# Encoder attention of a four-layer graph network: one-bank sum tiles, four row-term buffers, five blocks masked a part earlier, and a bfloat16 mask

## The chip, the cores and the metric

The kernel runs on one core of a Trainium2 chip, in one launch. The metric is the device time of a run in microseconds (us); less is better. The trace gives the time on a clock that starts with the span of one profiled execution. The engines are named as in the profile: PE (TensorE's matrix multiplications; PEld loads its weights), DVE (VectorE), ACT (ScalarE), POOL (GpSimd) and SP (SyncE, which here only issues DMAs). L469 is line 469 of the kernel before.

## The reference

Four residual layers on N = 2708 nodes with 512 features, over one dense 0/1 adjacency `adj` of 2708 x 2708; each is followed by a layer norm. Only the first one's attention matters here. It has four heads of 128 features, and the call passes `adj` for both patterns, so the two masked softmaxes are equal:

```python
Xw = jnp.einsum('hnd,hde->hne', Xh, W)
f1 = jnp.einsum('hnd,hd->hn', Xw, V[:, 0, :, 0])
f2 = jnp.einsum('hnd,hd->hn', Xw, V[:, 1, :, 0])
sig = jax.nn.sigmoid(f1[:, :, None] + f2[:, None, :])
...
local_att = _masked_softmax(local_pattern[None] * sig, lmask)
...
Xa = jnp.einsum('hij,hjd->hid', att, Xw)
```

After it come a batch norm, a block with a matrix multiplication, a decoder that uses the same `att`, and the layers 1 to 3, which the change leaves alone.

## The kernel before

**Tiling.** Everything is float32. The attention is computed transposed: the neighbours j lie on the 128 partitions, the nodes i along the free dimension. The nodes are cut into two halves of 1354 (`HSPAN`), the heads into two pairs, which makes four *parts* in the order `PARTS` = (half 0, pair 0), (0, 1), (1, 0), (1, 1). In every part a loop goes over 22 blocks of 128 neighbours (`ORDER`; one block has only 20 rows and stands in the middle). So there are 88 steps (`STEPS`), k = 0 to 87, and parts begin at 0, 22, 44 and 66.

**One step** has these pieces:

- A DMA on SP loads the block of `adj`, transposed (`adjT`), into a tile `a` of 128 x 1354 (four buffers). For pair 0 this is the raw 0/1 block, and it is masked (*prepared*): L423 writes z = (a == 0) into one tile `z`, L424 adds z times -1e30 to `a`, both on DVE, and a DMA on POOL's queue stores the result in `adj_d` in DRAM. For pair 1 the masked block is loaded back from `adj_d`.
- `tanhs` (L369): two ACT operations, tanh((f1 + f2) / 2), one for each head. f2 is the bias of each partition. f1, the *row term*, is read from a tile `f1b` of 128 x 1354, in which one row is spread to all partitions.
- `arguments` (L364): one DVE operation over both heads, (t + 1) times `a`.
- `exponentials` (L440): one ACT operation over both heads. For some blocks the result is stored for the decoder (`kept`, 1.35 MB, POOL's queue).
- `node_sums` (L469): for each head 11 matrix multiplications, one for each 128 nodes, with the exponentials as weights and 129 columns of values (the last is 1 and gives the softmax's sum). A float32 multiplication leaves two records, so a step has 44. They run two steps behind (`FRONT`).

**Sums.** The 11 results of a head need four PSUM banks (three to a bank), so two heads fill all eight. They are kept in three tiles `po0`, `po1`, `po2` of two banks each, which hold bank 0, 1 and 2 of both heads, and two tiles `psm0`, `psm1` of one bank for the last two results of each head. All of PSUM belongs to one pool, `ps_a`; the opening work uses the same tiles.

**Change of parts.** After the last sums of a part, `keep` evicts the eight banks on DVE (L684 takes a maximum, L685 a reciprocal, L686 writes the scaled `rows`), which only then leaves PSUM to the next part. Its function `turn` then transposes the rows on PE (L705, L713), again through the four banks `po[1]` of head 1, and copies them into `ft` on DVE or ACT (L726); `sm` goes to `rs_d` for the decoder. Until the transposes of both heads are done (`turns`), the new part's sums stand back (`waiting`). Statistics of `ft` (L728) are computed later, one in a step, in parts with pair 1 (`later`). After part 4 the evicted rows are transposed in the closing work, beside a few products of the weights of layer 3.

**Row terms.** Three buffers of tag `f1b` are turned over. Each part takes two; the buffer that a part's second tile takes was used until the last `tanhs` of the part before:

```python
                    with behind(loads[-9]):
                        nc.sync.dma_start(state["f1b"][0][:, :w], f1[:, 0, :])
                    nc.scalar.dma_start(state["f1b"][1][:, :w], f1[:, 1, :])
```

The first is loaded on SP's queue, the second on ACT's own. The row terms themselves are made at the start: `f1_rows` copies (L273) a chunk of 452 or 450 nodes out of PSUM. The three chunks of the first half are needed at once. The three of the second half come in `rest`, after the arguments of step 0: each is copied into a tile `f1c` (tag `rs`, two buffers) and stored to `f1_d` by a DMA on POOL's queue.

**Order.** Tile pools hand out buffers and insert the waits; a scheduler orders instructions on each engine by priority, and `behind(x)` or `tc.issue_after(x)` holds a group back behind a given instruction. The mask of step k stands behind the arguments of step k - 2 (`args[-2:-1]`), the arguments behind the previous ones, the `tanhs` behind the exponential of step k - 2.

## Time and profile before

| | us |
|---|---|
| median of 3 runs (3160.28 to 3168.04) | 3165.48 |
| the profiled execution | 3166.74 |
| its span in the trace | 3164.9 |
| up to the first steps (0 to 38.4 of the trace) | 38.4 |
| the 88 steps, until the last sum (38.4 to 528.4) | 490.0 |
| everything after it (closing work, decoder, layers 1 to 3) | 2636.5 |

Over the whole span PE is busy 3091.0 us (98%), DVE 2042.2 (65%), ACT 1368.7 (43%) and POOL 161.5 (5%). That average mixes stages: within the 88 steps PE is busy 453.0 of 490.0 us, DVE 392.4 and ACT 440.9, afterwards PE 2607.2 of 2636.5. An answer such as `L273 ... [6.25 <-DMA f_d<-f1c]` reads: line, engine, operation, output <- input with shapes, and in brackets how long the engine had been idle just before and what ended this (here a DMA that reads `f1c` and writes `f_d`, which is the trace's name for `f1_d`). In the timeline the line begins with start and duration in us.

### The profile page before, as it was taken

What the parts mean: (1) busy time and instruction counts of PE and PEld (TensorE: products, weight loads), DVE (VectorE), ACT (ScalarE), POOL (GpSimd) and SP (SyncE); (2) the same over time, 40 slices, a digit from 0 to 9 for tenths busy, and PEclk for the clock granted to TensorE, in tenths of its full rate; (3) what the DMA queues carried; (4) which work ended last, traced back from release to release, by engine and by line L of the source; (5) the groups of instructions that cost most, each with busy time, mean ns of one, the idle gap of its engine ahead of it and who ended that gap; (6) DMA issues with size and microseconds to landing.
All of it is one profiled execution on the core that took longest, in us unless ns stands there. A gap on an engine that the chain in (4) does not pass through costs nothing.

```text
span 3164.9 us, 39531 instructions
## 1 busy us (share of the span) xinstructions
PE 3091.0 (98%) x15144; PEld 2352.3 (74%) x15144; DVE 2042.2 (65%) x3807; ACT 1368.7 (43%) x1652; POOL 161.5 (5%) x282
## 2 busy tenths in 40 slices
PE   8999999999999999999999999999999999999999
PEld 7889988444444446885578888777768888888886
DVE  6968966876786685444266667777545555555565
ACT  6989988677867451001133333434301111111111
POOL 1100100000000000000011110000110000000000
PEclk9999999999999999999999999999999999999999
DMA  8866865156545413541154445556431111111110
GB/s 259 304 225 246 286 241 183 70 190 211 178 174 195 164 60 105 145 125 38 45 150 141 139 147 146 163 176 177 131 98 40 50 53 50 50 50 50 50 48 32
DMA packets 204307, 426.07 MB, mean 135 GB/s; under 512 B 21342, under 2 KB 135106, under 8 KB 198294
## 3 DMA queue, kind: packets, MB, share of 16 engines
q1 hardware_dynamic: 180126, 320.19, 33.1%
q0 software_dynamic: 23552, 101.26, 8.9%
q8 instruction: 119, 1.95, 0.3%
q10 hardware_dynamic: 440, 2.10, 0.2%
q14 instruction: 70, 0.57, 0.1%
HBM read 326.14 MB, written 95.87 MB: 133 GB/s over the span
## 4 chain that ended last, share of the span: by engine, by line
PE 72%; DVE 9%; ACT 9%; issue 7%; DMA 3%; POOL 0%; SPq 0%; DVEq 0%; POOLq 0%; ACTq 0%
PE po L1629 19%; PE ps_s L1424 18%; PE po L567 9%; PE ps_nb L1227 7%; PE ps_wide L1277 4%; ACT t L440 4%; DVE t L364 4%; ACT t L369 3%; PE po L469 3%; PE ps_hid L131 2%; PE ps_sup L1835 2%; PE ps_v L131 2%; PE ps_dec L994 2%; DMA f1b<-f_d 1%; PE ps_mlp L865 1%
## 5 line engine op out<-in xcount | busy, mean ns | idle before, releaser
L364 DVE SCALAR_TENSOR_TENSOR t<-t,a 128x2708 f32<-128x2708 f32 (+1 forms) x152 | 452.3, 2978 | 183.0 <-ACT t L369 178.4
L469 PE MATMUL po<-xw,t 128*128 128x129 f32 (+2 forms) x3872 | 448.5, 283 | 37.0 <-ACT t L440 21.8
L469 PEld LDWEIGHTS po<-xw,t 128*128 128x128 f32 (+2 forms) x3872 | 439.7, 193 | 45.4 <-ACT t L440 27.5
L369 ACT ACTIVATE t<-f1b,f2h 128x1354 f32<-128x1354 f32 (+1 forms) x304 | 415.8, 1413 | 43.5 <-PE po L567 32.8
L1424 PE MATMUL ps_s<-q,hT 128*128 128x256 f32 (+1 forms) x1848 | 405.5, 372 | 0.0
L1629 PE MATMUL po<-sup,e 128*128 128x256 f32 (+1 forms) x1512 | 398.3, 384 | 5.5 <-DVE c L1710 2.8
L567 PE MATMUL po<-t,emb 128*128 128x452 f32 (+3 forms) x1056 | 397.7, 545 | 4.4 <-ACT t L552 4.2
L1424 PEld LDWEIGHTS ps_s<-q,hT 128*128 128x128 f32 x1848 | 339.2, 190 | 49.8 <-issue 5.1
L567 PEld LDWEIGHTS po<-t,emb 128*128 128x128 f32 (+1 forms) x1056 | 193.4, 190 | 201.7 <-issue 188.4
L1629 PEld LDWEIGHTS po<-sup,e 128*128 128x128 f32 (+1 forms) x1512 | 264.4, 185 | 59.9 <-issue 19.4
L1629 PE MATMUL po<-held,T 128*128 128x256 f32 x1200 | 293.7, 380 | 0.0
L1629 PEld LDWEIGHTS po<-held,T 128*128 128x128 f32 x1200 | 226.8, 190 | 31.4 <-issue 0.9
L2030 DVE SCALAR_TENSOR_TENSOR e<-a_cols,ps_s 128x512 f32<-128x512 f32 (+1 forms) x121 | 79.9, 660 | 233.2 <-PE ps_s L1424 229.4
L440 ACT ACTIVATE t<-t 128x2708 f32<-128x2708 f32 x88 | 216.0, 2455 | 20.7 <-DVE t L364 20.0
L1424 PE MATMUL ps_s<-hT 128*128 128x256 f32 (+2 forms) x968 | 213.8, 372 | 0.7 <-ACT sup L1842 0.7
L1424 PEld LDWEIGHTS ps_s<-hT 128*128 128x128 f32 x968 | 175.0, 190 | 29.2 <-issue 4.3
L1227 PE MATMUL ps_nb<-hid_hi,at 128*128 128x512 f32 x484 | 185.5, 390 | 0.4 <-DVE at L1219 0.4
L552 ACT ACTIVATE t<-t 128x2708 f32<-128x2708 f32 x64 | 157.4, 2459 | 60.4 <-DVE t L364 60.2
L1227 PE MATMUL ps_nb<-hid_lo,at 128*128 128x512 f32 x462 | 179.9, 389 | 0.0
L1932 ACT ACTIVATE a_score<-a_score,neg_big 128x512 f32<-128x512 f32 (+3 forms) x131 | 88.6, 684 | 190.5 <-DMA a_score<-in_adjT_dram 95.7
L2022 ACT ACTIVATE q<-ps_wide,uq 128x256 f32<-128x256 f32 (+1 forms) x44 | 20.5, 466 | 335.7 <-PE ps_wide L1277 335.7
L1534 ACT ACTIVATE e<-e 128x512 f32<-128x512 f32 (+1 forms) x187 | 114.1, 617 | 118.1 <-DVE e L1533 117.8
(269 smaller groups left out, 3989.0 us busy)
## 6 DMA issues: line engine op xcount, KB each, us to landing
a<-adj_d SPq DMA_DIRECT2D x108, 677.0 KB
a_cols<-in_adjT_dram SPq DMA_DIRECT2D x200, 256.0 KB
a<-in_adjT_dram SPq DMA_DIRECT2D x42, 677.0 KB
adj_d<-a POOLq DMA_DIRECT2D x42, 677.0 KB, 5.5
kept<-t POOLq DMA_DIRECT2D x20, 1354.0 KB, 7.2
t<-kept SPq DMA_DIRECT2D x20, 1354.0 KB
raw<-in_adjT_dram SPq DMA_DIRECT2D x105, 256.0 KB
a_score<-in_adjT_dram SPq DMA_DIRECT2D x55, 256.0 KB
```

Source lines behind the costliest of these rows:

```text
L131: nc.tensor.matmul(ps[:n], xt[:, c, :n], w[:, c, :], start=(c == 0), stop=(c == C - 1))
L364: return nc.vector.scalar_tensor_tensor(t, t, GUARD, ab, ALU.add, ALU.mult)
L369: done = nc.scalar.activation(t[:, k, :], f1b[k][:n, :w], AF.Tanh, bias=f2h[:n, jt, h : h + 1], scale=0.5,)
L440: nc.scalar.activation(t[:rows, :, :w], t[:rows, :, :w], AF.Exp, scale=0.5)
L469: nc.tensor.matmul(po[k][b][:m, s * DR : (s + 1) * DR], t[own : own + n, k, i0 : i0 + m], values[own : own + n, jt, HP * p + k, :], start= ...
L552: nc.scalar.activation(t, t, AF.Exp, scale=0.5)
L567: nc.tensor.matmul(po[HB * k + q][:, :qw], values[r : r + n, jt, h * P : (h + 1) * P], t[r : r + n, k, q0 : q0 + qw], start=(place == 0), ...
L1227: nc.tensor.matmul(pos[it][:n], at, half[:, jt, :], start=(jt == 0 and k == 0), stop=(jt == NT - 1),)
L1277: nc.tensor.matmul(ps[:, :width], w(c, o), xt(c), start=(c == 0), stop=(c == C - 1),)
L1424: nc.tensor.matmul(ps[:, jb, i:w], keys[:, c, j : j + P], st["q"][:, c, i:], start=(c == 0), stop=(c == C - 1),)
L1534: return nc.scalar.activation(e, e, AF.Exp)
L1629: nc.tensor.matmul(po[bank][rows, half, :], lhsT, rhs, start=(k == 0 and half == 0) if first is None else first, stop=last, skip_group_che ...
```

## The change

It has five parts.

1. *Sums in eight one-bank tiles.* The opening work's PSUM pool is now `ps_p`. `banks()`, called after step 0's arguments, closes it and makes a pool `ps_a` with one tile for each bank of each head.
2. *Four row-term buffers.* `f1_tile` has two tags, `f1b0` and `f1b1`, of two buffers each; parts alternate between them. Both loads of a part are on SP's queue, behind the load of `a` three before.
3. *Row terms of the second half at the start.* The three chunks are copied into one tile `later_rows`, which is a spare `f1b1` buffer, and leave with one store instead of three.
4. *Mask.* `z` is bfloat16. The mask of step k stands behind the arguments of step k - 1 instead of k - 2.
5. *Five blocks of the second half masked during part 2.* At places 1, 4, 7, 10, 13 of part 2 `fetch_early` loads the raw block that is needed at place 2, 6, 10, 14, 18 of part 3 into a buffer of tag `f1b0`, whose tiles are idle in part 2. Three places later it is masked, behind the latest arguments, and stored to `adj_d`. In part 3 these five are loaded from `adj_d`, masked already.

The closing work's loads of `bq` and of one weight block move to tag `f1b0`. The diff, cut to its core:

```diff
...
     KEPT = [(8, 11, 14, 18), (1, 4, 7, 9, 11, 14, 17, 20)]
     KEPT = [[ORDER[k] for k in places] for places in KEPT]
+    EARLY = [1, 4, 7, 10, 13]
+    PREPARED = [ORDER[k] for k in (2, 6, 10, 14, 18)]
+    assert all(BLOCKS[jt][1] == P for jt in PREPARED)
     zeros = const.tile([P, NT, NHALF], F32, name="zeros")
     nc.vector.memset(zeros, 0.0)
     dram = ctx.enter_context(tc.tile_pool(name="dram", bufs=1, space=bass.MemoryType.DRAM))
...
         nc.vector.memset(xw[:, :, :, P:], 1.0)
         xT_sb = feat_tile("xT_sb")
 
+        def f1_tile(att, odd, name="f1b"):
+            return att.tile([P, HW], F32, tag=f"f1b{odd}", name=name, bufs=HP)
+
         def load_mlp(w, name):
             t = pf.tile([P, C, F], F32, tag="mlp_w", name=name)
             nc.sync.dma_start(t, w.rearrange("(c p) o -> p c o", p=P))
...
             nc.vector.tensor_copy(wv1, w0x[:, :, P : P + 1].to_broadcast([P, H, 32]))
 
-            stage, *f1b = [
-                att.tile([P, HW], F32, tag="f1b", name=name, bufs=HP + 1)
-                for name in ["f1_rows"] + ["f1b"] * HP
-            ]
+            stage, later_rows = [f1_tile(att, 1, name) for name in ("f1_rows", "f1_later")]
+            f1b = [f1_tile(att, 0) for _ in range(HP)]
             def f1_rows(ci, dst):
                 c0, w = CHUNKS[ci]
...
                 with tc.issue_after(step.ins):
                     for jt in range(AT_ONCE, NT):
                         values_of(jt)
-                    for ci in range(HB, NCH):
-                        c0, w = CHUNKS[ci]
-                        f1c = att.tile([P, BW], F32, tag="rs", name="f1c")
-                        f1_rows(ci, f1c)
-                        nc.gpsimd.dma_start(f1_d[:, c0 : c0 + w], f1c[0 : 32 * H : 32, :w])
+                    h0, w = HSPAN[1]
+                    for q, (q0, _) in enumerate(HCH[1]):
+                        f1_rows(HB + q, later_rows[:, q0:])
+                    nc.gpsimd.dma_start(f1_d[:, h0 : h0 + w], later_rows[0 : 32 * H : 32, :w])
                     copies(xw[:, NT - 1].rearrange("p h e -> p (h e)"))
                     copies(f2h[:, NT - 1, :])
                     nc.vector.tensor_scalar(bm1, prm_sb[:, MB_DEC, :], 1.0, None, ALU.subtract)
...
         PARTS = [(hf, p) for hf in range(NHALF) for p in range(H // HP)]
         STEPS = [(part, place) for part in PARTS for place in range(NT)]
 
-        def encoder_pass(values, att, psum, finish, f1b, blocks, spread, rest):
+        def encoder_pass(values, att, banks, finish, f1b, blocks, spread, rest):
             FRONT = 2
-            tanh, args, exps, tiles, loads = [], [], [], [], []
+            tanh, args, exps, tiles, loads, fetched = [], [], [], [], [], []
             state = {"f1b": f1b}
             def rows_of(k):
...
                 n = BLOCKS[jt][1]
                 return hf, p, jt, n if n == P else HR
 
+            def mask_block(a, hf, jt, rows, *after):
+
+                h0, w = HSPAN[hf]
+                j0, n = BLOCKS[jt]
+                z = att.tile([P, HW], BF16, tag="z", name="z", bufs=1)
+                with behind(*after):
+                    nc.vector.tensor_scalar(z[:rows, :w], a[:rows, :w], 0.0, None, ALU.is_equal)
+                done = nc.vector.scalar_tensor_tensor(
+                    a[:rows, :w], z[:rows, :w], -BIG, a[:rows, :w], ALU.mult, ALU.add
+                )
+                nc.gpsimd.dma_start(adj_d[j0 : j0 + n, h0 : h0 + w], a[:n, :w])
+                return done
+
+            def fetch_early(jt):
+
+                j0, n = BLOCKS[jt]
+                h0, w = HSPAN[1]
+                a = f1_tile(att, 0, "a_early")
+                with behind(loads[-1]):
+                    nc.sync.dma_start(a[:n, :w], adjT[j0 : j0 + n, h0 : h0 + w])
+                fetched.append((a, jt))
+
             def open_step(k):
                 hf, p, jt, rows = rows_of(k)
                 h0, w = HSPAN[hf]
                 j0, n = BLOCKS[jt]
-                prepare = p == 0
+                done_early = hf > 0 and jt in PREPARED
+                prepare = p == 0 and not done_early
                 if STEPS[k][1] == 0 and k > 0:
                     f1 = f1_d[HP * p : HP * (p + 1), h0 : h0 + w].partition_broadcast(P)
-                    state["f1b"] = [
-                        att.tile([P, HW], F32, tag="f1b", name="f1b", bufs=HP + 1)
-                        for _ in range(HP)
-                    ]
-                    with behind(loads[-9]):
-                        nc.sync.dma_start(state["f1b"][0][:, :w], f1[:, 0, :])
-                    nc.scalar.dma_start(state["f1b"][1][:, :w], f1[:, 1, :])
+                    state["f1b"] = [f1_tile(att, k // NT % 2) for _ in range(HP)]
+                    with behind(loads[-3]):
+                        for i in range(HP):
+                            nc.sync.dma_start(state["f1b"][i][:, :w], f1[:, i, :])
                 t = wide_tile(att, "t")[:, : HP * HW].rearrange("p (k w) -> p k w", k=HP)
                 src = adjT if prepare else adj_d
                 if k < len(blocks):
...
                 if n < P:
                     load_few(a, src, h0, w)
                 if prepare:
-                    z = att.tile([P, HW], F32, tag="z", name="z", bufs=1)
-                    with behind(*args[-2:-1]):
-                        nc.vector.tensor_scalar(z[:rows, :w], a[:rows, :w], 0.0, None, ALU.is_equal)
-                    nc.vector.scalar_tensor_tensor(
-                        a[:rows, :w], z[:rows, :w], -BIG, a[:rows, :w], ALU.mult, ALU.add
-                    )
-                    nc.gpsimd.dma_start(adj_d[j0 : j0 + n, h0 : h0 + w], a[:n, :w])
+                    mask_block(a, hf, jt, rows, *args[-1:])
                 tiles.append((t, a))
                 with behind(*exps[k - 2 : k - 1] if k > 1 else tanh[-1:]):
                     tanh.append(tanhs(t[:rows, :, :w], state["f1b"], hf, p, jt, rows, w))
...
                         skip_group_check=True,
                     )
 
-            both = [
-                psum.tile([P, HP, BANK], F32, tag=f"po{q}", name="po", bufs=1) for q in range(HB)
-            ]
-            more = [
-                psum.tile([P, BANK], F32, tag=f"psm{k}", name="po", bufs=1) for k in range(HP)
-            ]
-            po = [[both[q][:, k, :] for q in range(HB)] + [more[k]] for k in range(HP)]
-
             later, turns, waiting = [], [], []
             for k in range(len(STEPS) + FRONT):
                 inside, pending = k < len(STEPS), len(turns)
...
                     form(k)
                     if k == 0:
                         rest(args[0])
+                        po = banks()
                 if k >= FRONT:
                     part, place = STEPS[k - FRONT]
                     t, _ = tiles[k - FRONT]
...
                     exponentials(k - 1, *copies_done)
                 if inside and pending:
                     form(k, *copies_done if not scalar else [])
+                place = k - NT
+                if place - 3 in EARLY:
+                    a, jt = fetched.pop(0)
+                    args.append(mask_block(a, 1, jt, P, args[-1]))
+                if place in EARLY:
+                    fetch_early(PREPARED[EARLY.index(place)])
         def decoder_pass(values, att, psum, finish):
 
...
         less = p0.tile([P, C], F32, name="enc_less")
         with (
             tc.tile_pool(name="att_a", bufs=2) as att,
-            tc.tile_pool(name="ps_a", bufs=1, space=PSUM) as psum,
+            ExitStack() as sums,
         ):
+            first = ExitStack()
+            psum = first.enter_context(tc.tile_pool(name="ps_p", bufs=1, space=PSUM))
             f1b, blocks, spread, rest = project(att, psum)
+
+            def banks():
+
+                first.close()
+                pool = sums.enter_context(tc.tile_pool(name="ps_a", bufs=1, space=PSUM))
+                own = [
+                    [pool.tile([P, BANK], F32, name=f"po{k}{b}") for b in [HB, *range(HB)]]
+                    for k in range(HP)
+                ]
+                return [tiles[1:] + tiles[:1] for tiles in own]
+
             mlp_w, last_po, last_later, last_turn = [], [], [], []
             ft = feat_tile("ft")
 
...
                     return []
                 return [lambda *a, k=k: whole(k, *a) for k in range(HP)]
 
-            encoder_pass(xw, att, psum, keep, f1b, blocks, spread, rest)
+            encoder_pass(xw, att, banks, keep, f1b, blocks, spread, rest)
             emb = rows_tile("emb")
             room = emb[:, NT - 2 * C :, :]
             wqT, wkT = room[:, :C, :], room[:, C:, :]
...
             raws = []
             for name, w in (("wq", wq), ("wk", wk)):
                 for part in range(2):
-                    tag = "z" if len(raws) == 3 else "a"
-                    t = att.tile([P, HW], F32, tag=tag, name=name, bufs=1 if tag == "z" else 4)
+                    if len(raws) == 3:
+                        t = f1_tile(att, 0, name)
+                    else:
+                        t = att.tile([P, HW], F32, tag="a", name=name, bufs=4)
                     t = t[:, : half * F].rearrange("p (c o) -> p c o", c=half)
                     nc.sync.dma_start(
                         t,
...
                         ),
                     )
                     raws.append(t)
-            bq = att.tile([P, HW], F32, tag="f1b", name="bq", bufs=HP + 1)
+            bq = f1_tile(att, 0, "bq")
             nc.sync.dma_start(
                 bq[:, :F], bq_d.rearrange("c p -> (c p)").partition_broadcast(P)
             )
```

## Prediction

> **What bounds the kernel now.** The change touches only the encoder attention, so after the page I asked for busy time by stage: part 1 with its start, part 2, part 3, part 4, each cut where TensorE's sums run on without a gap after the change of parts.
>
> ```profile
> span 3164.9 us, 39531 instructions
> 38.40:184.20 145.80, 126.05 (x1038) 121.46 (x1038) 127.22 (x106) 119.13 (x73) 17.93 (x33) 0.93 0.78 261
> 184.20:301.30 117.10, 111.70 (x994) 110.99 (x993) 85.29 (x72) 112.85 (x73) 7.90 (x15) 0.97 0.68 241
> 301.30:426.90 125.60, 115.13 (x995) 113.11 (x993) 113.03 (x95) 112.01 (x70) 14.86 (x27) 0.96 0.77 276
> 426.90:528.40 101.50, 100.11 (x907) 99.68 (x906) 66.82 (x46) 96.88 (x60) 4.75 (x9) 0.98 0.60 208
> ```
>
> The columns are length, then PE, PEld, DVE, ACT and POOL busy, PE's clock, DMA share, GB/s. No engine has much room: the stage cannot gain more than some 10%, and DVE has slack only in parts 2 and 4. Next, who waits for whom in 38 to 530 us:
>
> ```profile
> ACT ft L726 <- PE po L705: 12.8, 4, 5.9
> PE po L469 <- DVE rows L686: 9.3, 3, 4.0
> ACT t L369 <- DMA f1b<-f_d: 8.9, 3, 4.2
> DVE f1c L273 <- DMA f_d<-f1c: 6.2, 1, 6.2
> ```
>
> All four sit at the start or where parts change. The timeline shows the pace between: first part 1, then part 2.
>
> ```profile
> 131.48 0.86 DVE L423 TENSOR_SCALAR z<-a 128x1354 f32<-128x1354 f32 x1
> 131.60 2.46 ACT L440 ACTIVATE t<-t 128x2708 f32<-128x2708 f32 x1 [0.47 <-DVE t L364]
> 132.38 1.57 DVE L424 SCALAR_TENSOR_TENSOR a<-z,a 128x1354 f32<-128x1354 f32 x1
> 134.08 2.98 DVE L364 SCALAR_TENSOR_TENSOR t<-t,a 128x2708 f32<-128x2708 f32 x1
> ...
> 195.01 2.45 ACT L440 ACTIVATE t<-t 128x2708 f32<-128x2708 f32 x1
> 195.14 2.98 DVE L364 SCALAR_TENSOR_TENSOR t<-t,a 128x2708 f32<-128x2708 f32 x1 [2.00 <-ACT t L369]
> ```
>
> In part 1 DVE is the bound: 0.86 + 1.57 + 2.98 and gaps make 5.49 us a step (128.59 to 134.08). In part 2, unmasked, ACT is: one exponential and two tanh, 4.98 us a step (190.03 to 195.01), and DVE idles 2.00 us in each. PE needs 44 records, under 4.94 us. Part 3 starts at ACT's pace, because the preceding slack let DVE mask ahead, and falls to DVE's later: exponentials at 342.85 and 347.83, but at 385.09 and 390.65. In all parts the last exponential is 8.4 us ahead of the last sum (519.9 against 528.35); I take that as kept, so what ACT gains, the end gains.
>
> **The change part by part.** I number the 88 steps 0 to 87, so that parts begin at 0, 22, 44, 66.
>
> Start. The third copy of the later rows waits for a buffer:
>
> ```profile
> 48.49 0.63 DVE L273 COPY f1c<-pf 128x450 f32<-128x450 f32 x1 [6.25 <-DMA f_d<-f1c]
> ```
>
> It now writes into a tile of its own, and that wait is gone. Not all is won: in the new order on DVE the mask of step 1 comes only after the arguments of step 0, where it had been free at 25.62. From 38.55 on: mask, the last copies, mask end at 42.45; arguments of step 1 to 45.5, mask of step 2, arguments of step 2 at 47.95 instead of 51.60: **3.6 gained**. Bounds: 6.2 if the mask hides again, 1 if step 1's store, now behind the row stores on POOL's queue, holds up a load (that load would land near 55, its mask is due near 62).
>
> Part 1's pace stays; the mask now writes bfloat16. The nearest rows are
>
> ```profile
> L942 DVE TENSOR_SCALAR linked<-rb 128x1354 bf16<-128x1354 f32 x2 | 1.9, 928 | 10.2 <-DMA rb<-rs_d 10.2
> L532 DVE TENSOR_SCALAR_CACHE_REDUCE z<-a 128x1354 uint8<-128x1354 f32 x42 | 65.6, 1562 | 3.5 <-DMA a<-adj_d 3.5
> ```
>
> The first is the same kind of compare from float32 to bfloat16, 0.88 and 0.98 us against 0.86; the second also sums, which explains its time. I take +0.04 for 21 masks: **-0.8**. Bounds per mask: 0 and +0.70. The second operation reads bfloat16 and float32, and I leave its 1.57.
>
> First change of parts (step 22). Now:
>
> ```profile
> 161.33 1.42 ACT L369 ACTIVATE t<-f1b,f2h 128x1354 f32<-128x1354 f32 x1 [3.91 <-DMA f1b<-f_d]
> ...
> 170.67 0.16 DVE L684 TENSOR_SCALAR rc<-po 128x3 f32<-128x3 f32 x1
> ...
> 174.61 4.26 PE L469 MATMUL po<-xw,t 128*128 128x129 f32 x22 [2.64 <-DVE rows L686]
> ...
> 185.03 2.47 ACT L440 ACTIVATE t<-t 128x2708 f32<-128x2708 f32 x1
> ```
>
> With four row buffers both loads are issued on SP some six steps ahead (0.7 MB each, 9.4 us at worst, two loads of `a` behind them, each with about 13 us to spare). The exponential of step 21 then starts at 159.15 instead of 162.66, and the arguments of step 23 end at 167.3 instead of 170.7, where the evictions start. They took 6.3 us; PE resumed 3.9 us after their start, when bank 0 of both heads was free. With one tile a bank it resumes after the first bank, 1.15 us in. The new order then interleaves transposes and copies: following it bank by bank with the evictions' spacing, the arguments of step 24 start 7.95 us after the evictions (10.7 before), PE runs on from 10.0 (13.5 before), and the exponential of step 24 starts at 11.75, that is at 179.05 instead of 185.03. **6.0**, of which I keep 5.5, because PE's clock fell after the gap shown above (windows of 2 us, clock third from the right):
>
> ```profile
> 172.00:174.00 2.00, 0.00 (x0) 0.00 (x0) 2.00 (x15) 2.00 (x2) 0.00 (x0) 1.00 0.79 303
> 176.00:178.00 2.00, 2.00 (x11) 2.00 (x10) 0.87 (x6) 1.70 (x2) 0.00 (x0) 0.50 0.83 347
> ```
>
> The clock halved after 2.64 us of idling, and 22 records took 4.26 us against 2.69 warm; the remaining gap is 1.9 us, for which no row decides, so the bounds are 0 and -1.6 at each change. [...]
>
> Part 2 takes on five masks of part 3. Each is 2.45 us on DVE where 2.00 is idle, so the next arguments start 0.45 late, 1.2 where a 0.69 us statistic lies in the same step. The exponential has 2.0 us of slack after its arguments (4.98 - 2.98), so I cost them at **0**; without that cover five times 1.2. Their DMAs: ten of 0.68 MB in 110 us, on a share of 0.68 where part 1 runs at 0.78. A fetch from the third on waits on SP for the store of the mask two before it, with later loads of `a` queued behind: issue is held by up to 5 us, and these loads have about 15. Bounds 0 and -10.
>
> Second change (step 44). No row wait is left to win (0.79 in the trace). Evictions start equally late, as two masks still precede them. PE gains 2.3, but step 46's exponential waits for the copy of a second sums tile, which stands on DVE behind the arguments of step 47: 14.95 us after the evictions' start against 13.98: **-0.8**. Bounds +2.3, -2.
>
> Part 3. Steps masked early cost DVE 2.98, the other ones 5.49. With 17 of 22 masked DVE needs 4.92 a step, below ACT's 4.98; three masked steps in a row fall 1.5 behind, within the 2.0. From the exponential of step 46 (302.97) to that of 64 (396.15) it took 93.2; 18 x 4.98 is 89.6: **3.5**. Third change: the exponential of step 65 comes at 405.45, 9.3 later, because of the second row load; 4.98 instead is **4.3**. After it, as at the first change, 14.2 becomes 11.75; less 1.0 because PE, now without slack, carries the backlog of the short last block: **1.5**.
>
> Closing. Head 0's banks can be evicted while PE still sums head 1 (some 2.4 us): **2**, bounds 0 and 3.
>
> Sum: 3.6 - 0.8 + 5.5 - 0.8 + 3.5 + 4.3 + 1.5 + 2 = 18.8. The profiled execution took 3166.74 (its span and 1.84 around), so 3147.9; the median of the three runs is 1.26 below it, so 3146.7, say **3147**.
>
> **The rivals.** [...] *Changes of parts give little*: the clock stays low in them and PE, waiting for DVE's interleaved copies, holds ACT. Then only the start, the two row waits (3.5, 4.3) and the pace remain: 14, less the second change's -2, or 3153. For it: 12.8 us of waiting for transposes in the trace, which the new order only shuffles. *Part 2's traffic is late*: 10 us lost, 3157. For it: a kept store of 1.35 MB lands beside each early one. That buffers do not do what they say is excluded: on ACT's queue the row loads are gone.
>
> **How the numbers follow.** Forecast (3142 to 3151) 0.60; changes give little 0.20; late traffic 0.12; slower masks 0.08. About 0.3%, 9.5 us, is what a measurement can tell from none: bounds 3156 and 3175. Faster: 0.60 + 0.18 and a quarter of the traffic's case, 0.81; slower: half of the last and a little for the unforeseen, 0.05; same 0.14. Range: from 3138 (the start at 6.2, no clock loss, the second change at its better end) to 3160 (past late traffic).
>
> **What would show it.** After: no wait of ACT for f1b; no wait of DVE for f_d; compare at 0.86 to 0.98; 4.98 between exponentials throughout part 3; last sum near 512. Wrong if part 2's exponentials are further apart than 4.98, if arguments wait for DMA there, or if PE's clock near steps 22 and 66 stays at 0.50 for longer than now.

## The result and the profile after

The changed kernel takes 3141.59 us (median of 6 runs, 3140.45 to 3144.70) against 3164.98 for the kernel before (median of 6). The ratio is 0.9929, with a 95% interval from 0.9916 to 0.9942: faster by 23 us. Forecast were 3147, between 3138 and 3160.

The profiled execution, cut at about the same events as before; the columns are those of the prediction's first table.

```profile
span 3141.4 us, 39518 instructions
38.40:173.40 135.00, 121.01 (x1045) 115.89 (x1041) 128.90 (x108) 119.56 (x73) 17.86 (x33) 0.97 0.85 297
173.40:291.00 117.60, 112.69 (x1007) 111.52 (x1008) 94.33 (x80) 112.00 (x71) 10.03 (x19) 0.99 0.78 280
291.00:406.00 115.00, 111.30 (x981) 109.74 (x980) 103.75 (x87) 111.66 (x70) 12.52 (x23) 0.97 0.77 279
406.00:508.00 102.00, 100.15 (x904) 99.79 (x905) 68.76 (x56) 96.38 (x59) 4.74 (x9) 0.98 0.60 207
```

Parts 1 and 3 are 10.8 and 10.6 us shorter, parts 2 and 4 keep their lengths, though VectorE now works 94.3 us in part 2 instead of 85.3: the early masks lie in its idle time. PE's clock in part 1 is 0.97 instead of 0.93. Next, what is waited for in 38 to 530 us (total, number of times, longest):

```profile
ACT ft L755 <- PE po L734: 9.2, 4, 2.7
PE po L486 <- DVE rc L713: 4.0, 2, 2.6
PE po L486 <- DVE f_later L277: 2.3, 1, 2.3
```

No wait of ACT for f1b and none of DVE for f_d is left. The third line stands at the start, where the sums of step 0 wait for the copies of the later rows; before, that took 5.2 us. PE's wait for the evictions fell from 9.3 to 4.0 us and now ends when the first bank is out (the profile names the small operation beside its `rows`), not with a later `rows`. The first change of parts shows it:

```profile
163.33 0.15 DVE L713 TENSOR_SCALAR rc<-po 128x3 f32<-128x3 f32 x1
...
164.44 2.25 PE L486 MATMUL po<-xw,t 128*128 128x129 f32 x18 [1.44 <-DVE rc L713]
...
174.20 2.46 ACT L457 ACTIVATE t<-t 128x2708 f32<-128x2708 f32 x1
```

PE resumes 1.11 us after the evictions' start (3.9 before), its 18 records take 2.25 us, so the clock is still up (1.00 in each window of 2 us from 160 to 170), and the exponential of step 24 follows 10.9 us after that start (14.4 before).

The gap between consecutive exponentials (L440, now L457) is the best ruler, since all 88 of them are in both traces; "before" and "after" are starts in us. The last row is the first product of the closing work (ps_m).

| step | before (gap) | after (gap) | after is ahead by |
|---|---|---|---|
| 1 | 41.63 (6.77) | 45.33 (10.41) | -3.70 |
| 2 | 54.61 (12.98) | 50.79 (5.46) | 3.82 |
| 20 | 153.64 (5.49) | 149.81 (5.49) | 3.83 |
| 21 | 162.66 (9.02) | 155.31 (5.50) | 7.35 |
| 24 | 185.03 (12.41) | 174.20 (8.92) | 10.83 |
| 43 | 280.62 (5.90) | 268.83 (4.98) | 11.79 |
| 46 | 302.97 (12.39) | 292.87 (14.08) | 10.10 |
| 64 | 396.15 (5.50) | 382.53 (4.98) | 13.62 |
| 65 | 405.45 (9.30) | 387.51 (4.98) | 17.94 |
| 68 | 427.75 (12.33) | 406.70 (9.23) | 21.05 |
| 87 | 520.59 (3.14) | 499.49 (3.14) | 21.10 |
| ps_m | 540.00 | 517.48 | 22.52 |

The spans differ by 23.5, the medians by 23.4. What follows ps_m took between 2621.8 and 2625.3 us in all the profiles of this document, whatever the edit. So differences of a few us are read from the steps, and the times only confirm them.

Between the last exponential and ps_m one thing is mixed in. In part 4 PE idles behind the short block, its records are slower for a while after that in most of the profiles, and PE catches up hardly 0.1 us a step afterwards (in the changed kernel 3.4 us at a clock of 0.50 cost 1.7, and ten steps later 1.06 of that is left against experiment 10). What it lost is still there at the last sum. Here are the 440 records from the short block to the end of the part in the changed kernel, in experiment 3 and in experiment 10:

```profile
459.01 50.98 PE L486 MATMUL po<-xw,t 128*128 128x129 f32 x440 [1.85 <-ACT t L457]
```

```profile
457.86 52.28 PE L486 MATMUL po<-xw,t 128*128 128x129 f32 x440 [1.86 <-ACT t L457]
```

```profile
455.01 49.92 PE L486 MATMUL po<-xw,t 128*128 128x129 f32 x440 [1.33 <-ACT t L457]
```

The clock was at 0.50 for 3.4 us in the first (460.4 to 463.8). In the second it was down for some 6 us, by an estimate from its records: the first 82 took 12.36 us, at the 0.114 us each of part 2 in the changed kernel, where the clock was at 1.00, they would take 9.3, and the 3.0 us between are half of the time at half speed. The third is as short as those 440 records of part 2 (49.99). From the start of the last exponential to the end of the last sum it took 10.20 us in the kernel before and in experiment 5, 10.5 in the changed kernel and experiments 4, 6 and 7, 11.4 to 11.8 in experiments 2, 3, 8 and 9, but 9.44 in experiments 1, 10 and 11. So ps_m carries up to 2.4 us that are put down to PE's clock in part 4 and do not come from what an edit was made for.

### The profile page after: what moved, and what is told of

It reads as the page before. It is cut to its first block, busy times and chain, and to the rows that moved or that the text cites. A ratio compares the mean times of both kernels' runs of the same rounds, so it can differ in the third digit from the quotient of the medians.

```text
span 3141.4 us, 39518 instructions
## 1 busy us (share of the span) xinstructions
PE 3081.8 (98%) x15144; PEld 2344.5 (75%) x15144; DVE 2040.9 (65%) x3807; ACT 1365.8 (43%) x1652; POOL 159.7 (5%) x280
## 3 DMA queue, kind: packets, MB, share of 16 engines
q8 instruction: 119, 1.95, 0.3%
## 4 chain that ended last, share of the span: by engine, by line
PE 77%; ACT 10%; DVE 9%; issue 2%; DMA 2%; SPq 0%; DVEq 0%; ACTq 0%
PE po L1660 20%; PE ps_s L1455 18%; PE po L583 9%; PE ps_nb L1258 7%; PE ps_wide L1308 5%; ACT t L457 4%; ACT t L372 4%; PE po L486 4%; DVE t L367 3%; PE ps_sup L1866 2%; PE ps_hid L131 2%; PE ps_v L131 2%; PE ps_dec L1025 2%; PE ps_mlp L896 1%; PE ps_e L1588 1%
## 5 line engine op out<-in xcount | busy, mean ns | idle before, releaser
L486 PE MATMUL po<-xw,t 128*128 128x129 f32 (+2 forms) x3872 | 440.4, 280 | 23.7 <-ACT t L457 16.7
L486 PEld LDWEIGHTS po<-xw,t 128*128 128x128 f32 (+2 forms) x3872 | 431.7, 190 | 31.9 <-ACT t L457 21.8
L457 ACT ACTIVATE t<-t 128x2708 f32<-128x2708 f32 x88 | 215.7, 2451 | 14.6 <-DVE t L367 13.9
```

What stands on the lines that cost most here:

```text
L457: nc.scalar.activation(t[:rows, :, :w], t[:rows, :, :w], AF.Exp, scale=0.5)
L486: nc.tensor.matmul(po[k][b][:m, s * DR : (s + 1) * DR], t[own : own + n, k, i0 : i0 + m], values[own : own + n, jt, HP * p + k, :], start= ...
```

## Experiments

Here are all of them at a glance; the last column says how much earlier than in the kernel before (540.00) the first product of the closing work starts, the clock's share just told included.

| kernel | ratio to before (95%) | gaps before steps 24, 46, 68 | ps_m earlier by |
|---|---|---|---|
| changed kernel | 0.9929 (0.9916, 0.9942) | 8.92, 14.08, 9.23 | 22.5 |
| 1: with two-bank tiles | 0.9952 (0.9938, 0.9967) | 11.71, 13.25, 10.23 | 18.5 |
| 2: without early masks | 0.9961 (0.9947, 0.9976) | 8.91, 12.73, 8.85 | 15.8 |
| 3: mask two behind | 0.9934 (0.9920, 0.9949) | 8.92, 12.11, 8.86 | 22.4 |
| 4: float32 mask | 0.9934 (0.9917, 0.9951) | 8.92, 13.25, 9.15 | 23.7 |
| 5: before, third f1c buffer | 0.9981 (0.9972, 0.9990) | 12.02, 12.40, 12.18 | 7.2 |
| 6: before, four row buffers | 0.9979 (0.9969, 0.9988) | 11.63, 14.79, 12.86 | 5.7 |
| 7: before, one-bank tiles | 0.9979 (0.9969, 0.9988) | 9.66, 12.42, 9.52 | 7.8 |
| 8: four edits more | 0.9896 (0.9881, 0.9911) | 8.38, 8.31, 8.34 | 31.5 |
| 9: 3 with split row loads | 0.9916 (0.9899, 0.9932) | 8.91, 12.10, 8.85 | 25.1 |
| 10: six blocks and sm | 0.9909 (0.9894, 0.9924) | 8.38, 10.63, 8.32 | 28.1 |
| 11: 8 with GpSimd compares | 0.9966 (0.9954, 0.9978) | 8.11, 8.39, 8.50 | 10.6 |

**1. Two-bank tiles again.**

```diff
-                own = [
-                    [pool.tile([P, BANK], F32, name=f"po{k}{b}") for b in [HB, *range(HB)]]
-                    for k in range(HP)
-                ]
-                return [tiles[1:] + tiles[:1] for tiles in own]
+                both = [pool.tile([P, HP, BANK], F32, name=f"po{q}") for q in range(HB)]
+                more = [pool.tile([P, BANK], F32, name=f"psm{k}") for k in range(HP)]
+                return [[both[q][:, k, :] for q in range(HB)] + [more[k]] for k in range(HP)]
```

> The changed kernel with the sums' tiles as they were before (three tiles of two banks, two of one), everything else kept. Theory A (one tile a bank lets TensorE start on the first evicted bank, and this makes the changes of parts shorter): the gaps between the exponentials of steps 23 and 24 and of steps 67 and 68 go back from 8.92 and 9.23 to about 12.4 us, the gap before step 46 falls from 14.08 to about 12.4, and the closing loses 2.4: some 7 us slower than the changed kernel. Theory B (the shorter changes come from the row loads and from the masks' new places, not from the banks): all three gaps stay within 1 us of the changed kernel, and so does the time.

The first gap went back by 2.8 us, the third by 1.0, the second fell by 0.8, and the closing lost 0.7: 4.0 in this trace. Theory A's direction held, its 7 us did not in the profile; the profiled execution was the fastest of its four (3145.17, median 3148.80), and the ratios do put some 7 us between the two kernels. PE's clock explains 1.9 of the 3 us that are missing. At the second change PE was at full speed (16 records in 2.02 us after 2.70 us of idling; 18 took 3.82 in the changed kernel), which is the 0.8 there and not an effect of the banks. In part 4 it lost nothing behind the short block (18 records in 2.28 us), 1.06 us less than the changed kernel. From the end of the last sum to ps_m it took 9.21 us instead of 7.49, so that the banks are worth 1.7 in the closing. At the first change PE waits 3.72 us, longer than in the kernel before (2.64), and comes back slowly:

```profile
167.07 3.89 PE L486 MATMUL po<-xw,t 128*128 128x129 f32 x18 [3.72 <-DVE rows L713]
```

The same 18 records took 2.25 us in the changed kernel.

**2. No early masks.**

```diff
-    EARLY = [1, 4, 7, 10, 13]
-    PREPARED = [ORDER[k] for k in (2, 6, 10, 14, 18)]
+    EARLY = []
+    PREPARED = []
```

> The changed kernel without the five early masks: every block of the second half is masked in part 3. Theory A (early masks are free in part 2 and give part 3 the pace of ScalarE): part 2 stays at 4.98 us a step, part 3 falls back to 5.49 from about step 58 on and its exponential of step 64 comes 3.5 us or more later against that of step 46; with the mask of step 46 back in the second change of parts, that gap grows by up to 2.4 more: 3.5 to 6 us slower. Theory B (part 2 pays for them: DMAs and VectorE): part 2 gets shorter by 1 us or more, which takes back a part of the 3.5.

Part 2 stayed at 4.98 us a step, so the early masks cost nothing there, and theory B falls. Part 3 fell to 5.5 us a step already from step 52 on, not 58: from step 46 to 65 it took 101.99 us instead of 94.64, that is 7.35 more. The gap before step 46 did not grow but fell by 1.4. Until the last exponential 5.8 us were lost, within the range of theory A; until ps_m 6.7, with 0.9 us in part 4 that are put down to the clock (the first 24 records behind the short block took 5.49 us). A part of the 1.4 is PE's clock too: it came back at full speed there (18 records in 2.25 us after 1.61 us of idling, 3.82 in the changed kernel).

**3. The mask two behind.**

```diff
-                    mask_block(a, hf, jt, rows, *args[-1:])
+                    mask_block(a, hf, jt, rows, *args[-2:-1])
```

> The changed kernel with the mask of step k behind the arguments of step k-2 again instead of k-1. Theory A (the new place of the mask costs the start the part of the wait that did not come back): the mask of step 1 runs near 26 us of the trace, the arguments of step 1 start near 40 instead of 42.31, the exponential of step 1 comes 2.4 us earlier and all later ones keep this; 2.4 us faster unless the second change of parts, where a mask now may stand ahead of more work, takes it back (0 to 2.5). Theory B (the start is bound by something else than the mask, such as TensorE's sums of step 0): the exponential of step 1 stays at 45.3, no gain.

The start gained what theory A says (step 1 at 42.00, gap 6.76; step 2 at 48.66 and the later ones of parts 1 and 2 2.1 earlier than in the changed kernel), and the second change another 2.0. But 2.93 us were lost at step 63, and 0.3 at step 64. There VectorE waits for a load of `a`, which SP issues 12 us after the two row loads. In the kernel's order that load waits for the store of the masked block that used its buffer last. That store was issued at 354.02, beside both row loads, and SP could issue the load only at 365.06, 10.3 us after the store's issue ended; of the eight such stores issued from 335 to 380 the median landed 5.4 us after its issue. First SP, then VectorE:

```profile
352.69 2.42 SPq L430 DMA_DIRECT2D f1b<-f_d  x2
365.06 2.86 SPq L439 DMA_DIRECT2D a<-in_adjT_dram  x2
```

```profile
371.07 0.87 DVE L402 TENSOR_SCALAR z<-a 128x1354 bf16<-128x1354 f32 x1 [3.70 <-DMA a<-in_adjT_dram]
```

The last exponential is 1.15 us earlier than in the changed kernel, ps_m 0.15 later: PE lost the difference in part 4, behind the short block (52.28 against 50.98 us above). So the kernel is no faster, and what theory A promised for the whole did not come.

**4. A float32 mask.**

```diff
-                z = att.tile([P, HW], BF16, tag="z", name="z", bufs=1)
+                z = att.tile([P, HW], F32, tag="z", name="z", bufs=1)
```

> The changed kernel with the mask in float32. The instructions on VectorE keep their order. Theory A (the output's type costs nothing: steps of part 1 are 5.49 us apart in both kernels): compare 0.86 us, part 1 at 5.49 us a step, time unchanged within 1 us. Theory B (the forecast's 0.04 us a mask): 0.8 us faster, which the distances of the exponentials in part 1 would show. A slow form of the compare (0.7 us a mask) would have been seen in the changed kernel and is not expected.

Theory A: the compare takes 860 ns on average in float32 and 859 in bfloat16, part 1 has the same 5.49, and L403 takes 1.57 in both. This kernel has the changed kernel's order of instructions, and yet its second gap is 13.25 instead of 14.08. What differs is PE there, which is told under experiment 10.

**5. The kernel before with a third f1c buffer.**

```diff
-                        f1c = att.tile([P, BW], F32, tag="rs", name="f1c")
+                        f1c = att.tile([P, BW], F32, tag="rs", name="f1c", bufs=3)
```

> The kernel before with one edit: a third f1c buffer, so that the copy at L273 need not wait for a store. Theory A (the wait of 6.25 us is on the path and the mask of step 1 comes back into the idle time before): the exponential of step 2 at about 48.6 instead of 54.61, all later steps keep the 6.0 us: 6 us faster than before. Theory B (what the changed kernel won there, 3.8, is all that there is, the rest turning into a wait of TensorE or ScalarE): 3.8.

Step 2 came at 48.17 instead of 54.61: 6.4 us, which are kept (7.2 at ps_m). Theory A. The changed kernel has only 3.8 of it.

**6. The kernel before with the row-term buffers alone.** The core of the edit:

```diff
-                    with behind(loads[-9]):
-                        nc.sync.dma_start(state["f1b"][0][:, :w], f1[:, 0, :])
-                    nc.scalar.dma_start(state["f1b"][1][:, :w], f1[:, 1, :])
+                    state["f1b"] = [f1_tile(att, k // NT % 2) for _ in range(HP)]
+                    with behind(loads[-3]):
+                        for i in range(HP):
+                            nc.sync.dma_start(state["f1b"][i][:, :w], f1[:, i, :])
```

> The kernel before with the row-term buffers alone changed: two tags of two buffers, both loads on SP's queue behind the load three before, and the bfloat16 mask that makes room. Theory A (the three waits of ScalarE for a row term are on the path and add up): the gaps before the exponentials of steps 21, 43 and 65 fall from 9.02, 5.90 and 9.30 to 5.5, 4.98 and 5.5: 8.2 to 8.8 us faster. Theory B (what ScalarE no longer waits is waited for again at the change of parts, because TensorE or VectorE set its end): the gaps before steps 24, 46 and 68 grow by as much as the others fall, and less than half of the 8.8 remains.

The gaps before steps 21, 43 and 65 fell to 5.49, 4.98 and 5.49, by 8.3 in all, as theory A says. The gaps at the changes of parts then changed by -0.8, +2.4 and +0.5, so that 6.0 remained at the last exponential: between the theories, nearer A. Of the +2.4, 0.6 us is that the evictions start later against the exponential of step 45 (1.06 us ahead of it instead of 1.66). The other 1.8 come after their start: PE idled 4.59 us (4.01 before), its first 16 records took 3.78 us (3.43 before, where the clock was at 0.50 from 291.8 to 295.2), and VectorE waited 1.42 us for a transpose.

**7. The kernel before with one-bank tiles alone.** `banks()` of the changed kernel, and nothing else.

> The kernel before with the one-bank tiles alone. Theory A (as taking them out of the changed kernel showed: 2.8 at the first change of parts, nothing or a small loss at the second, 1.0 at the third, 0.7 in the closing): 3 to 4.5 us faster, with the gaps before steps 24 and 68 near 9.6 and 11.3. Theory B (the banks need the other parts of the change): gaps of 12 us as before, 0 to 1 us.

Gaps of 9.66, 12.42 and 9.52, and 1.4 in the closing (from the last exponential to ps_m 17.99 instead of 19.41: 1.7 less from the end of the last sum on, 0.3 more before it): 7.8 us by the trace: 2.8 at each of the outer changes, 1.4 in the closing and the rest in small pieces. More than theory A, and B falls. The banks need nothing else of the change.

**8. Four more edits.**

```diff
-    EARLY = [1, 4, 7, 10, 13]
-    PREPARED = [ORDER[k] for k in (2, 6, 10, 14, 18)]
+    EARLY = [0, 2, 5, 7, 10, 13]
+    PREPARED = [ORDER[k] for k in (2, 3, 4, 9, 13, 17)]
...
-                    with behind(loads[-3]):
-                        for i in range(HP):
+                    for i in range(HP):
+                        with behind(loads[-3 * (HP - i) - 3 if p else -3]):
                             nc.sync.dma_start(state["f1b"][i][:, :w], f1[:, i, :])
...
-                    mask_block(a, hf, jt, rows, *args[-1:])
+                    mask_block(a, hf, jt, rows, *args[-2:-1])
...
-                        nc.vector.tensor_copy(sm, bank[:NB, BANK - P :])
+                        copy(sm, bank[:NB, BANK - P :])
```

> The changed kernel with four more edits: the mask of step k behind the arguments of step k-2; six early blocks, for places 2, 3, 4, 9, 13, 17 of part 3, fetched at places 0, 2, 5, 7, 10, 13 of part 2; the small copy sm on the engine that copies ft; the row loads of parts 2 and 4 behind the loads nine and six before. Theory A (what was left of the start is the mask of step 1; at the second change the masks and sm stand in VectorE's queue ahead of the last rows; with the mask two behind, step 63 waited because both row loads and two stores went out at once): exponential of step 2 at 48.6, the gap before step 46 falls from 14.08 to about 10, no gap near step 63, pace of part 3 4.98 save 1 us: 6 to 8 us faster than the changed kernel, near 3135. Theory B (six fetches in part 2 and three early masks in a row at the start of part 3 cost as much as they give: loads late in part 2, 5.49 a step in part 3's second half): no gain over the changed kernel beyond the start's 2.3.

3133.15 us, ratio 0.9896: the fastest kernel here, and more than theory A expected. Step 2 is at 48.29, the gap before step 46 is 8.31, part 3 keeps 4.98 throughout.

**9. The third kernel with split row loads.** The third of the edits just shown, added to the third kernel.

> The kernel with the mask two behind (the third experiment) with one further edit: the row loads of parts 2 and 4 behind the loads nine and six before, one at a time, instead of both behind the third before. Theory A (step 63 waited 2.84 us because the load of a for step 64 had to wait for a store that shared the DMA engines with both row loads and a kept store): the gap before step 63 falls from 7.91 to 5.0 and all later exponentials come 2.9 us earlier. Theory B (the mask standing ahead of the arguments is itself the cause, whatever the DMAs do): the gap stays, or turns up at a neighbouring step.

Gap before step 63: 4.98 instead of 7.91; ps_m 2.7 earlier than without the split. The compare that waited 3.70 us for its load in experiment 3 starts there without a wait (368.14). Theory A.

**10. Six blocks and sm.** The first and the last of the four edits, the mask one behind.

> The changed kernel with two of the last kernel's edits, the six early blocks (places 2, 3, 4, 9, 13, 17) and sm on the engine that copies ft; the masks stay one behind. Theory A (the gap before step 46 is long because a mask and sm stand in VectorE's queue ahead of the second head's last rows and copies): it falls from 14.08 to 8 to 9 us, as with all four edits (8.31), while the start keeps its 10.41 before step 1; 5 to 6 us faster than the changed kernel. Theory B (that gain came from the masks' place two behind): the gap stays above 11.

Between the theories: the gap before step 46 fell from 14.08 to 10.63, not to 8 or 9, and with the mask two behind as well it is 8.31. Two things make up the other 2.3 us, the first of them 1.15 and the second, by what is left, 1.17. First, with the mask one behind, a mask stands directly ahead of the arguments after which the evictions begin, so these start 0.80 us before the exponential of step 45; two behind they start 1.95 before it, 1.15 earlier. Second, PE's clock. PE waits here 2.60 us for the evictions and its 18 records then take 3.36 us (first line), in the kernel of experiment 8 it waits 0.58 and they take 2.25 (second line; the clock was at 1.00 from 274 to 278).

```profile
278.92 3.36 PE L486 MATMUL po<-xw,t 128*128 128x129 f32 x18 [2.60 <-DVE rc L713]
```

```profile
274.93 2.25 PE L486 MATMUL po<-xw,t 128*128 128x129 f32 x18 [0.58 <-DVE rc L713]
```

How large the clock's part is, experiment 4 tells. It has the changed kernel's order, but in its trace PE came through the middle of part 2 more slowly. From the short block to the end of the part PE runs on without a gap:

```profile
226.51 49.99 PE L486 MATMUL po<-xw,t 128*128 128x129 f32 x440 [1.86 <-ACT t L457]
```

That is the changed kernel; in experiment 4 the same 440 records took 50.98 us, since the clock was down at their beginning (0.88 in the window from 224 to 228, 0.69 in that from 228 to 232, which makes about 3.4 us at 0.50; 1.00 in both in the changed kernel). So PE came later to the end of the part, waited 1.60 instead of 2.59 us for the evictions, and came back at full speed (18 records in 2.25 us instead of 3.82): 13.25 instead of 14.08, or 0.8 us for the clock. In the changed kernel these 0.8 us are a wait of VectorE for a transpose, ahead of `sm`; in experiment 4 there is none:

```profile
287.40 0.28 DVE L744 COPY sm<-po 11x128 f32<-11x128 f32 x1 [0.75 <-PE po L742]
```

Between experiment 4 and experiment 3, both at full speed there, lie 1.14 us, which is the mask's place alone. The 1.17 in experiment 10 are put down to the clock without such a pair: no profile has its order at full speed.

**11. Compares on GpSimd.**

```diff
+                pool = hf == 0 and 2 < ORDER.index(jt) < NT and ORDER.index(jt) % 2
-                z = att.tile([P, HW], BF16, tag="z", name="z", bufs=1)
+                z = att.tile([P, HW], BF16, tag="zp" if pool else "z", name="z", bufs=1)
                 with behind(*after):
-                    nc.vector.tensor_scalar(z[:rows, :w], a[:rows, :w], 0.0, None, ALU.is_equal)
+                    (nc.gpsimd if pool else nc.vector).tensor_scalar(...)
```

> The kernel with all four edits, with the compare of every second mask of part 1 (odd places from 3 on) moved to GpSimd, with a z of its own. Theory A (GpSimd is idle and its compare is through within a step): VectorE has 0.86 us less in every second step, part 1 runs at 5.06 us a step and ten steps give some 8 us. Theory B (GpSimd is slower than the step, or slows VectorE while it runs): the steps with a compare on GpSimd get longer than 5.49 and the kernel loses, by any amount up to the compare's length for each of them.

Theory B: ps_m 20.8 us later than in experiment 8. GpSimd's compare took 3.63 to 10.16 us, and VectorE's own was stretched beside it, as one pair shows, GpSimd first:

```profile
64.65 5.72 POOL L403 TENSOR_SCALAR z<-a 128x1354 bf16<-128x1354 f32 x1
```

```profile
66.80 4.30 DVE L403 TENSOR_SCALAR z<-a 128x1354 bf16<-128x1354 f32 x1
```

## Why the prediction was right, step by step

The mechanism and its places were right but for the second change, and each of the eight terms can be read from the steps:

| term | forecast | measured |
|---|---|---|
| start | 3.6 | 3.8 (step 2) |
| bfloat16, 21 masks | -0.8 | 0.0 (steps 2 to 20) |
| first change, with its row wait | 5.5 | 7.0 (3.5 at step 21, 3.5 at step 24) |
| masks in part 2 | 0 | 0 |
| second change | -0.8 | -0.8 (0.9 at step 43, -1.7 at step 46) |
| pace of part 3 | 3.5 | 3.5 (13.62 - 10.10) |
| third row wait | 4.3 | 4.3 (step 65) |
| third change | 1.5 | 3.1 (step 68) |
| closing | 2 | 1.4 (1.7 from the last sum on, -0.3 before it) |
| sum, before rounding | 18.8 | 22.4 |

**Where sizes were off.** Three terms were too low, together by 3.9 us, and the sum by 3.6. The median lies 5.1 below 3146.7 and so 0.4 below 3142, the lower end of what the prediction called its forecast, though within its range; the other 1.5 us are what follows ps_m (1.0 less in these two profiles) and the spread of the runs. The first change: followed bank by bank it came to 6.0, of which 0.5 was kept back for the slow clock. PE then idled 1.44 us, not 1.9, came back at full speed, and the exponential of step 24 stood 10.9 us after the evictions' start instead of 11.75. The third change: the same 11.75 and another 1.0 for the backlog of the short last block were assumed; it was 11.2 (evictions from 395.52, exponential at 406.70). The bfloat16 term: 0.04 a mask was taken from L942, two compares of the same form in another stage (0.88 and 0.98 us); experiment 4 shows it to be nothing.

The closing was 0.6 too high. From the end of the last sum to ps_m it took 7.49 us instead of 9.21, that is 1.7; the rest was lost ahead of it. There the prediction misread the trace: the last exponential starts at 520.59 and the last sum ends at 530.8, not 519.9 and 528.35 (the table ahead of the prediction also ends the steps too early, at 528.4). The distance is 10.20 us there and 9.31, 7.67 and 9.26 in the parts before, not 8.4 in each. That it is kept held here to 0.3 us, by luck: between the kernels of this document it goes from 9.44 to 11.80, with the clock behind the short block.

**What was right for a narrower reason than given.** The pace of part 3 gave 3.5, but experiment 2 shows that the early masks are worth 6.7 in the changed kernel. The mask one behind keeps VectorE from masking ahead, so without them the pace breaks at step 52, not 58; the early masks pay for that first. In the same way the start gave 3.8 of the 6.4 that a third f1c buffer alone gives (experiment 5); the prediction saw this loss in the order of instructions, and experiment 3 confirms it (bound 6.2). At the second change the -0.8 was luck: errors cancelled. The row wait gave 0.9 (step 43), where nothing was expected, and the gap grew by 1.7. Half of that is a step that the prediction had wrong: the evictions do not start equally late but 0.80 us ahead of the exponential of step 45 instead of 1.66, so 0.86 later, because the mask one behind stands directly ahead of the arguments before them. The other half is the clock. From the evictions' start to the exponential of step 46 it took 14.05 us in the kernel before, 14.89 in the changed one and again 14.05 in experiment 4, where the clock stayed up. So the 14.95 came true through the clock, not through the order of the copies, which already stood behind the arguments of step 47 in the kernel before. Nor did it help there that PE resumes earlier: with two-bank tiles and the clock up (experiment 1) it is 14.05 as well.

**The single parts** give 7.2 (start), 5.7 (row buffers) and 7.8 us (banks) on the kernel before, and the early masks 6.7 on the changed one: 27.4 against 22.5 together. The mask's place accounts for a part of the difference: 2.6 at the start, and the pace that the early masks first have to restore (6.8 against the 3.5 that the kernel before had to win from step 46 to 64). What PE's clock happened to do is in all these numbers.

**The rivals.** Slower masks, which had 0.08 at a bound of 0.70 us each: excluded by 859 ns on average, against 860 in float32 (experiment 4). Little at the changes of parts: wrong at the first and third, true of the second, where the order of VectorE's queue held ScalarE. Late traffic in part 2: part 2 ran at 4.98 throughout. Yet the danger was real one part later: with masks running one step further ahead, two row loads at once did hold up a load of `a` (experiments 3 and 9). The changed kernel did not meet it because it also needs its loads later.

## What to carry to other kernels

Measure a change of many parts on a repeating event that both traces have, here the exponentials: terms of 1 to 7 us can be read from the distances of the steps, which agree to 0.1 us in most places, where the times differ by 3 us and more from run to run. Two things have to be looked at first: where the counting starts (step 0 itself began between 34.65 and 35.81 us here), and where PE's clock may have fallen, which was worth 0.8 us at the second change and up to 2.4 at the end. A buffer that takes away a wait moves work forward, and what was hidden in the wait (here a mask, later a load behind row loads) must be given a new place, or a part of the gain is lost. Where engines hand over to each other, look at what stands in the queue directly ahead of the first instruction that the waiting engine needs: moving the masks and a copy of 0.27 us out of the way took 5.8 us from a gap of 14.08, some 0.8 to 1.2 of it through the clock.

## What the runs showed of the hardware

**PE's clock after an idle time.** At the changes of parts the sums resumed at full speed (18 records in 2.25 us, the clock at 1.00 from 164 to 168 in the changed kernel) after 1.44 to 1.61 us of idling wherever that happened. After 2.59 to 2.74 us it went either way: 18 records in 3.82 (changed kernel) and 3.36 us (experiment 10), but 16 in 2.16 after 2.70 us and 22 in 2.83 after 2.64 (both experiment 5, with the clock at 1.00 in the windows from 286 to 288 and from 170 to 172, where another 2.64 was followed by 22 in 4.39). After 3.71 us and more it was slow each time (22 in 5.07 after 3.71 in experiment 6, 18 in 3.89 after 3.72 in experiment 1, 16 in 3.43 after 4.01 in the kernel before). Behind the short block (records of 20 rows only) less was enough: in part 2 the clock fell after 1.86 us in experiment 4 (0.69 from 228 to 232) and not in the changed kernel (1.00), and after 1.33 us in experiment 8 (0.50 from 224 to 226) and not in experiment 10, where the 440 records after it took 49.99 us as in the changed kernel. In the changed kernel the windows at the second change show it, clock third from the right:

```profile
276.00:278.00 2.00, 0.50 (x5) 0.27 (x3) 2.00 (x2) 2.00 (x3) 0.00 (x0) 1.00 0.86 349
278.00:280.00 2.00, 0.91 (x6) 0.94 (x7) 2.00 (x13) 2.00 (x2) 0.00 (x0) 0.88 0.89 238
280.00:282.00 2.00, 2.00 (x11) 2.00 (x11) 2.00 (x15) 1.23 (x1) 0.00 (x0) 0.50 0.96 326
```

So one profile of such a place is one draw; why the same idle time is followed now by the one and now by the other, no run shows. In the profiles of the kernel before and of the changed one, each stretch at 0.50 within the 88 steps lasted 3.4 us (ten of them) or 6.8 us (four).

**VectorE beside GpSimd.** In experiment 11 VectorE's compare started in GpSimd's, took 4.30 us instead of 0.86 and ended 0.7 us after it; the arguments beside such a compare took 5.26 us once instead of 2.98, and the longest GpSimd compare took 10.16 us where the shortest took 3.63. VectorE's compare ended about one compare of its own (0.86) after GpSimd's. The arguments ended 2.3 us after GpSimd's compare, less than their own 2.98. What holds VectorE up in such a pair, no run shows.
